# A selective-scan and attention kernel: ScalarE scales the turned dt*u out of PSUM from an earlier unit on, and the fold of Wq and Wk moves to the second image

## The chip, the core and the metric

The kernel runs on one core of a Trainium2 chip. The metric is the device time of one launch in microseconds (us); lower is better. The engines are named as the profile names them: PE is TensorE (matmuls, and PEld its weight loads), DVE is VectorE, ACT is ScalarE, POOL is GpSimd, and SP is the engine whose queue issues the DMAs.

## The reference

Four images of 384 channels and 32x32 positions pass through a state-space layer (four directions k, 16 states per channel) and then through attention and a mixture of four experts. What matters here is the scan and the attention scores:

```python
def step(h, inp):
    dtt, ut, bt, ct = inp
    dA = jnp.exp(dtt[..., None] * A)
    h = h * dA + (dtt * ut)[..., None] * bt[:, :, None, :]
    y = jnp.einsum('bkdn,bkn->bkd', h, ct)
    return (h, y)
...
q = jnp.einsum('btc,ch->bth', x, Wq)
k = jnp.einsum('btc,ch->bth', x, Wk)
wei = jnp.einsum('bth,bsh->bts', q, k) * scale
```

Since q times k transposed is x (Wq Wk^T) x^T, the kernel computes the product of the two weights once. That is the fold.

## The kernel before

**Units and ticks.** The scan is cut into 768 units, 192 for each image (`IMAGE`). A unit is 32 channels times 4 states on the 128 partitions, and 1024 positions along the free dimension. The units of an image run over the channel block m (3), the direction k (4, in two pairs), the group of four states q (4), and the 32-channel block j (4). So 16 units in a row (`EACH`) share one pair (k, m), and four in a row (`NJ`) share one q.

The main loop counts ticks. In tick t it writes out, in this order: `decay(t + 2)` (ACT, L550, the exponential da of the unit after the next), deferred work, `front(t)` (DVE, L557, v = du * B into PSUM), `turned(t + 1)` (PE, L815), `back(t - 1)` (POOL, L570, h * C), `middle(t)` (DVE, L563, the scan), on every fourth tick `row(t - 2)` (PE, L595, the sum over states into y, 16 matmuls), `fetch(t)` (the DMAs of later units), one step of the preparation of an image, and then `go_on`, which steps the generators in the list `side` and the one in `waiting` (attention and experts of the image before). A generator that yields `"wait", n` is not stepped again for n ticks. The order is written out by hand (`manual_schedule`), so each engine executes its instructions in the order in which these ticks issue them, and a tick is a place in that order, not a time. The buffers of da are three, so the da issued in tick t is written only when the scan of unit t - 1 is done. The buffers of v are two.

**Two ways to v.** In the first image, half of the groups of four units (q = 1 and q = 3) can get v in a way that spares DVE. The generator `feed` (L748) loads du of a (k, m) from memory, turns it on PE in 128x128 blocks (L780), copies it from PSUM into the tile dut (ACT, L782), and then lets ACT scale dut by B, 32 instructions of 128x128 for a group of four units (L798), eight of them in a tick, into a tile st. `turned` (L815) then transposes st back on PE, eight transposes a unit, straight into v. `feed` starts a group n0 (its first unit) only if the clock has not passed n0 - 5 (`AHEAD`), and at most two st tiles are alive, so that a group is started from tick n0 - 12 on. A unit that has no st when `turned` is called gets its v from DVE as usual. In the kernel before, the first group so treated is that of unit 36.

**The fold.** `fold` (L706) loads Wq and Wk, turns them (PE L720, ACT L724, six times), multiplies them (PE L730, ACT L735, three times) and stores the result to `g_d` (L738). It is in `side` from tick 0, and its last line appends `feed`. So `feed` begins when the fold has ended. Its tiles come from the pool of st.

**Preparation.** `preparation(b)` normalises image b, projects it (`project_x`, L382), and computes dt and du for each of six (m, pair) in `project_dt` (L407): twice two matmuls into two PSUM banks that must be free in the same tick, a Softplus on ACT for each (with a table load there and one back for Exp), two products on DVE, and four stores. In the first image's ticks there are two such banks (`FIRST_BANKS`) for preparation, fold and `feed` together; the bank's `give` makes it free in the same tick. From tick 192 on there are four, and pools for the attention's tiles (`a0`, `ht`) take the place of that of st.

**What follows an image.** When the last `row` of an image is out, `evict` starts `finish` (layer norm, Gelu, residual), and `behind` waits for it and runs `attention` (L843), which first loads `g_d`, and `experts`.

The call that decides the order of fold and feed is

```python
side.append(later())
side.append(fold())
decay(0)
decay(1)
```

Of the kernel before, what the change touches and what calls it, by code (L numbers as in the profile page):

```python
# [8 lines left out]
F32 = mybir.dt.float32  # L9
AF = mybir.ActivationFunctionType  # L10
# [5 lines left out]
P = 128  # L16
B = 4
C = 384
M = C // P
HW = 32  # L20
L = HW * HW
NH = L // 512
K = 4
N = 16
# [8 lines left out]
NI = P // DJ  # L33
# [16 lines left out]
def hybrid_kernel(  # L50
# [22 lines left out]
    nc = tc.nc  # L73
# [16 lines left out]
    first = ExitStack()  # L90
    pools = {
        "st": first.enter_context(tc.tile_pool(name="stp", bufs=2)),
        "dut": first.enter_context(tc.tile_pool(name="dutp", bufs=1)),
        "v": first.enter_context(tc.tile_pool(name="ps_v", bufs=2, space=PSUM)),
        "pm": ps_m,
    }
# [285 lines left out]
    def project_x(b, pair, u, xd):  # L382

        name = f"bc_{b}_{pair}"
        bc = yield from slots.take(name, P, L)
        mine = slice(64 * pair, 64 * pair + 64)
        other = slice(64 - 64 * pair, 128 - 64 * pair)
        for h in range(NH):
            s = bass.ts(h, 512)
            ps = yield from banks.take(f"pxd_{b}_{pair}_{h}")  # L390
            for c in range(M):
                nc.tensor.matmul(
                    ps, wx[:, c, pair, :], u[c][:, s], start=(c == 0), stop=(c == M - 1)
                )
            yield "wait", 1
            nc.scalar.copy(half(xd[mine, :], h, pair), ps[mine, :].rearrange("p (h w) -> p h w", w=HW))
            rows = half(bc[other, :], h, pair), ps[other, :].rearrange("p (h w) -> p h w", w=HW)
            if b == 0 and pair == 0:
                nc.vector.tensor_copy(*rows)
            else:  # L400
                nc.scalar.copy(*rows)
            banks.give(f"pxd_{b}_{pair}_{h}")
        yield "wait", 1
        nc.sync.dma_start(rows_d[b, pair].rearrange("k j n l -> (k j n) l"), bc[other, :])
        slots.give(name)

    def project_dt(b, pair, m, u, xd):  # L407
# [217 lines left out]
    def layernorm(dst, src, name, lag, b=0, into=None):  # L625
# [77 lines left out]
            banks.give(f"rb_{name}_{h}")  # L703
        return dst

    def fold():  # L706

        raw = pools["st"].tile([P, 2, M, C], F32, tag="st", name="w_raw")
        for j, w in enumerate((wq, wk)):
            nc.sync.dma_start(raw[:, j], w.rearrange("(c p) d -> p c d", p=P))
        wt = pools["st"].tile([P, 2, M, C], F32, tag="st", name="w_t")
        yield "wait", 3
        for j in range(2):
            for d in range(M):
                ps = yield from banks.take(f"pwt_{j}_{d}")
                for c in range(M):
                    nc.tensor.transpose(  # L720
                        ps[:, c * P : (c + 1) * P], raw[:, j, c, d * P : (d + 1) * P], ident
                    )
                yield "wait", 1
                nc.scalar.copy(wt[:, j, d, :], ps[:, :C])  # L724
                banks.give(f"pwt_{j}_{d}")
        g = pools["st"].tile([P, M, C], F32, tag="st", name="g_s")
# [12 lines left out]
        side.append(feed())  # L739

    stored_du = set()
    scaled = {}
    NT = L // P

    def feed():  # L748
        bt = one.tile([P, 2, NT, 4 * N], F32, tag="fx0", name="bt")
        for pair in range(2):  # L750
# [12 lines left out]
            slots.give(f"bt_{pair}")  # L763
        begun = []
        for n in range(0, IMAGE, EACH):
            u = units[n]
            if clock[0] > n + EACH - NJ - AHEAD:
                continue
            while (u["k"], u["m"]) not in stored_du:
                yield "wait", 1  # L770
            name = f"turn_{u['name']}"
            du = yield from slots.take(name, P, L)
            nc.sync.dma_start(du, dts_d[0, u["k"]][1, u["m"] * P : (u["m"] + 1) * P, :])
            yield "wait", 2
            dut = pools["dut"].tile([P, NT, P], F32, tag="dut", name=f"dut_{n}")
            for h in range(2):
                ps = yield from banks.take(f"{name}_{h}")
                for t in range(4):
                    o = (4 * h + t) * P
                    nc.tensor.transpose(ps[:, t * P : (t + 1) * P], du[:, o : o + P], ident)  # L780
                yield "wait", 1
                nc.scalar.copy(dut[:, 4 * h : 4 * h + 4, :], ps.rearrange("p (t d) -> p t d", t=4))  # L782
                banks.give(f"{name}_{h}")
            slots.give(name)
            for q in range(1, NQ, 2):
                n0 = n + q * NJ
                if clock[0] > n0 - AHEAD:
                    continue
                while len(begun) >= 2 and clock[0] < begun[-2] + NJ:

                    yield "wait", 1
                if clock[0] > n0 - AHEAD:
                    continue
                begun.append(n0)
                st = pools["st"].tile([P, NT, NJ * P], F32, tag="st", name=f"st_{n0}")
                for t in range(NT):
                    for i in range(NI):
                        nc.scalar.activation(  # L798
                            st[:, t, :].rearrange("p (d i) -> p i d", i=NI)[:, i, :], dut[:, t, :],
                            AF.Copy,  # L800
                            scale=bt[:, u["pair"], t, u["i"] * 2 * N + q * NI + i :][:, :1],
                        )
                    if t % 2:
                        yield "wait", 1
                scaled[n0] = st

    def turned(n):

# [32 lines left out]
            defer(1 + m // 2, add)  # L841

    def attention(b, yb, fx0):  # L843
        gw_ = []
        for name, w in ((f"wg_{b}", g_d), (f"wv_{b}", wv.rearrange("(c p) d -> p c d", p=P))):
            ta = yield from slots.take(f"{name}a", P, 2, C)
# [433 lines left out]
    assert clock[0] < -2  # L1280
    clock[0] = -2
    side.append(later())
    side.append(fold())
    decay(0)
    decay(1)
    t = 0
    while t < NU + 4 or waiting or side or due or inner or parked:
        clock[0] = t
        if t + 2 < NU:
            decay(t + 2)  # L1290
        for f in due.pop(t, []):
# [78 lines left out]
```

## Time and profile before

The median of three runs is 3821.93 us (3818.68 to 3824.02). The profiled execution took 3819.22 us, with a span of 3817.4 us.

| stretch of the span | what runs | us | DVE busy | ACT busy | PE busy | granted PE clock |
|---|---|---|---|---|---|---|
| 49.37 to 171.99 | units 0 to 31 | 122.62 | 116.02 | 70.64 | 69.73 | 0.64 |
| 171.99 to 715.92 | units 32 to 191 | 543.93 | 493.31 | 462.10 | 344.07 | 0.69 |
| 715.92 to 781.50 | first units of the second image | 65.58 | 63.88 | 37.94 | 41.56 | 0.68 |

The stretches begin and end at the start of a scan (L563). Each engine's share says how much of a stretch it had an instruction in work; it says nothing of whether another engine waited for it. Over the whole span, 768 scans took 1751.6 us of DVE, 688 products v another 854.3 us, and 640 scaling instructions (L798) were put down with 498 ns each in the median. In 80 units, then, v was made by way of st.

An entry such as "DVE h L563 <- PE v L815: 20.2, 16, 3.7" in a view of waits means that the scan stood idle for 20.2 us in total, 16 times, 3.7 us at the longest, until the transposes of line 815 released it.

### The profile page before, as it was taken

The numbers are of one execution on the slowest core, as the hardware profiler recorded it, in microseconds if no ns is written. First come the engines' busy times: TensorE is split into PE (matmuls) and PEld (weight loads), VectorE is DVE, ScalarE is ACT, GpSimd is POOL, SyncE is SP. The second block draws the span as 40 slices with busy tenths as digits, with TensorE's granted clock in tenths as the row PEclk, the third lists the DMA queues.
The fourth block names the chain that finished last, engine by engine and source line by source line (L and its number), as shares of the span: only waits on it lengthen the run. The fifth ranks groups of instructions, "written<-read, shape, count | busy, mean of one in ns | idle before, by whom it ended". The sixth has DMA issues, their size and how long they took to land.

```text
span 3817.4 us, 33900 instructions
## 1 busy us (share of the span) xinstructions
PE 3373.4 (88%) x11367; PEld 1498.2 (39%) x11367; DVE 2993.1 (78%) x2094; ACT 2104.3 (55%) x2695; POOL 1816.5 (48%) x776
## 2 busy tenths in 40 slices
PE   4665666679999999799999999789999999999999
PEld 1123322235334334345333343354343434644444
DVE  6999899999899999989988999999999992210000
ACT  4688888555666656556565555455555552422121
POOL 2677677645555555545555565455666560000000
PEclk7677766689999999899999999899999999999999
DMA  6565556445576666536756656346566551222321
GB/s 205 204 224 177 213 203 219 171 167 186 179 247 227 222 238 226 178 120 209 239 195 224 214 194 208 136 151 208 200 205 235 188 181 38 90 73 84 94 84 52
DMA packets 407838, 678.26 MB, mean 178 GB/s; under 512 B 33472, under 2 KB 280560, under 8 KB 407664
## 3 DMA queue, kind: packets, MB, share of 16 engines
q1 hardware_dynamic: 401456, 675.70, 51.9%
q8 instruction: 90, 1.47, 0.2%
q10 hardware_dynamic: 6208, 0.39, 0.1%
q14 instruction: 84, 0.69, 0.1%
HBM read 604.04 MB, written 71.96 MB: 177 GB/s over the span
## 4 chain that ended last, share of the span: by engine, by line
PE 42%; DVE 34%; ACT 6%; issue 5%; DMA 1%; POOL 1%; DVEq 0%; SPq 0%; POOLq 0%; ACTq 0%
DVE h L563 21%; PE ph L1154 15%; PE fy L1179 15%; DVE v L557 10%; PE y L595 4%; ACT da L550 2%; PE pq L868 2%; PE pv L879 2%; PE ss L897 1%; ACT st L798 1%; PE po L963 1%; DVE fy L1188 1%; POOL h L570 1%; PE v L815 1%; DMA du<-dts 1%
## 5 line engine op out<-in xcount | busy, mean ns | idle before, releaser
L570 POOL TENSOR_TENSOR h<-h,bc 128x1024 f32<-128x1024 f32 x768 | 1815.5, 2367 | 1330.7 <-DVE v L557 1099.3
L563 DVE TENSOR_TENSOR_SCAN h<-da,v 128x1024 f32<-128x1024 f32 x768 | 1751.6, 2284 | 106.4 <-PE v L815 20.2
L550 ACT ACTIVATE da<-dt,a 128x1024 f32<-128x1024 f32 x768 | 876.1, 1146 | 940.9 <-DVE h L563 892.0
L1154 PE MATMUL ph<-fx,w 128*128 128x512 f32 x2304 | 1020.7, 599 | 7.3 <-DMA w<-in_w 3.2
L1179 PE MATMUL fy<-ht,w 128*128 128x512 f32 x2304 | 1023.2, 601 | 0.9 <-ACT dt L429 0.9
L557 DVE TENSOR_TENSOR v<-du,bc 128x1024 f32<-128x1024 f32 x688 | 854.3, 1242 | 35.8 <-DMA du<-dts 16.3
L1179 PEld LDWEIGHTS fy<-ht,w 128*128 128x128 f32 x2304 | 437.4, 192 | 577.0 <-issue 550.0
L1154 PEld LDWEIGHTS ph<-fx,w 128*128 128x128 f32 x2304 | 433.5, 191 | 581.6 <-issue 533.5
L595 PE MATMUL y<-h,sel 128*32 128x512 f32 x3072 | 536.7, 675 | 140.5 <-POOL h L570 140.5
L1139 ACT ACTIVATE ht<-ph,b1s 128x512 f32<-128x512 f32 x384 | 257.6, 678 | 456.7 <-PE ph L1154 455.9
L1188 DVE SCALAR_TENSOR_TENSOR fy<-fy,b2s,tw 128x512 f32<-128x512 f32 x96 | 72.2, 752 | 426.1 <-PE fy L1179 426.1
L595 PEld LDWEIGHTS y<-h,sel 128*32 128x32 f32 x3072 | 102.0, 117 | 481.3 <-POOL h L570 252.2
L815 PE MATMUL v<-ident,st 128*128 128x128 f32 x640 | 134.3, 381 | 97.9 <-DVE h L563 96.3
L798 ACT ACTIVATE st<-dut,bt 128x128 f32<-128x128 f32 x640 | 205.1, 501 | 0.1
L1143 ACT ACTIVATE ht<-ht 128x3072 f32<-128x3072 f32 x64 | 176.8, 2763 | 0.8
L815 PEld LDWEIGHTS v<-ident,st 128*128 128x128 f32 x640 | 109.2, 199 | 161.2 <-issue 86.2
L550 ACT ACT_TABLE_LOAD x110 | 141.1, 1283 | 14.5 <-DMA dt<-dts 11.5
L423 PE MATMUL pdt<-xd,wdt 12*128 12x512 f32 x184 | 84.2, 819 | 66.4 <-ACT dt L429 34.9
L963 PE MATMUL po<-pt,vt 128*128 128x256 f32 x480 | 106.1, 370 | 7.8 <-ACT pt L859 7.8
L897 PE MATMUL ss<-axn,qt 128*128 128x512 f32 (+3 forms) x288 | 100.5, 493 | 3.1 <-ACT pr L915 2.7
L963 PEld LDWEIGHTS po<-pt,vt 128*128 128x128 f32 x480 | 93.8, 196 | 23.4 <-ACT pt L859 10.0
L911 DVE TENSOR_REDUCE nb<-ss 128x1 f32<-128x512 f32 (+3 forms) x48 | 25.9, 552 | 75.3 <-PE ss L902 61.0
(201 smaller groups left out, 1642.6 us busy)
## 6 DMA issues: line engine op xcount, KB each, us to landing
bc<-rows SPq DMA_DIRECT2D x384, 512.0 KB, 4.7
w<-in_w SPq DMA_DIRECT2D x384, 384.0 KB, 6.0
dt<-dts SPq DMA_DIRECT2D x192, 512.0 KB, 4.0
du<-dts SPq DMA_DIRECT2D x192, 512.0 KB, 6.6
dts<-dt SPq DMA_DIRECT2D x48, 512.0 KB, 3.5
dts<-du SPq DMA_DIRECT2D x48, 512.0 KB, 3.7
fx<-t2d SPq DMA_DIRECT2D x12, 768.0 KB, 6.4
tw<-mkd SPq DMA_DIRECT2D x32, 256.0 KB, 6.5
```

The costliest lines, as they stand in the source:

```text
L550: nc.scalar.activation(u["da"], spread["dt4", n], AF.Exp, scale=a4[:, g, u["q"] : u["q"] + 1])
L557: return nc.vector.tensor_tensor(u["v"], spread["du4", n], spread["bc", n][:, 0, :], ALU.mult)
L563: nc.vector.tensor_tensor_scan(u["h"][:, ::step], u["da"][:, ::step], u["v"][:, ::step], 0.0, op0=ALU.mult, op1=ALU.add,)
L570: product = nc.gpsimd.tensor_tensor(h, h, spread["bc", n][:, 1, :], ALU.mult)
L595: nc.tensor.matmul(y, sel, h, start=first, stop=last, tile_position=(0, jj * DJ))
L798: nc.scalar.activation(st[:, t, :].rearrange("p (d i) -> p i d", i=NI)[:, i, :], dut[:, t, :], AF.Copy, scale=bt[:, u["pair"], t, u["i"] * ...
L815: nc.tensor.transpose(u["v"][:, t * P : (t + 1) * P], st[:, t, u["j"] * P : (u["j"] + 1) * P], ident)
L963: nc.tensor.matmul(pv[:, o:], vt[:, j, m * P : (m + 1) * P], pts[step][j // 4][:, j % 4, o:], start=False, stop=(j == nj - 1),)
L1139: nc.scalar.activation(ht[:, f, :], ps, AF.Identity, bias=bias)
L1143: nc.scalar.activation(ht, ht, AF.Gelu)
L1154: nc.tensor.matmul(ps, tiles[n][:, c, (f % 2) * P : (f % 2 + 1) * P], xns[h][:, c, :], start=(c == 0), stop=(c == M - 1),)
L1179: nc.tensor.matmul(pss[m], tiles[n][:, f, :], hts[fh][:, f, :], start=(fh == 0 and f == 0), stop=(fh == 1 and f == FH - 1),)
```

## The change

Four edits, made together:

1. `feed` is put into `side` at the start in place of `fold`. It waits for its own inputs instead: `stored_rows` says that the projected rows of a pair are stored, and each pair's rows are turned when they are first needed (`turn_rows`).
2. The tile dut and its copy are gone. For each group q, du is turned again on PE into a bank, four blocks at a time, and ACT scales the blocks out of that bank. The first bank is held over one tick of waiting and two of scaling, the second is taken in the middle of the first one's scaling if it is free. The slot with du is held until both groups of a (k, m) are done.
3. `fold` is put into `side` at tick 192. Its tiles come from the pool `ht`, it waits two ticks for its loads in place of three, and it ends by noting itself in `folded`.
4. `attention` waits until `folded` is set.

```diff
+        if b == 0:
+            stored_rows.add(pair)
...
-        raw = pools["st"].tile([P, 2, M, C], F32, tag="st", name="w_raw")
+        def square(name):
+            t = pools["ht"].tile([P, M, L], F32, tag="ht", name=name)
+            t = t.rearrange("p m l -> p (m l)")[:, : 2 * M * C]
+            return t.rearrange("p (j c d) -> p j c d", j=2, c=M)
+
+        raw = square("w_raw")
...
-        yield "wait", 3
+        wt = square("w_t")
+        yield "wait", 2
...
-        side.append(feed())
+        folded.append(1)
...
-            dut = pools["dut"].tile([P, NT, P], F32, tag="dut", name=f"dut_{n}")
-            for h in range(2):
-                ps = yield from banks.take(f"{name}_{h}")
+
+            def dut(q, h, du=du, name=name):
+                ps = banks.now(f"{name}_{q}_{h}")
                 for t in range(4):
                     o = (4 * h + t) * P
                     nc.tensor.transpose(ps[:, t * P : (t + 1) * P], du[:, o : o + P], ident)
-                yield "wait", 1
-                nc.scalar.copy(dut[:, 4 * h : 4 * h + 4, :], ps.rearrange("p (t d) -> p t d", t=4))
-                banks.give(f"{name}_{h}")
-            slots.give(name)
+                return ps
...
-                for t in range(NT):
-                    for i in range(NI):
-                        nc.scalar.activation(
-                            st[:, t, :].rearrange("p (d i) -> p i d", i=NI)[:, i, :], dut[:, t, :],
-                            AF.Copy,
-                            scale=bt[:, u["pair"], t, u["i"] * 2 * N + q * NI + i :][:, :1],
-                        )
-                    if t % 2:
+                ps = [None, None]
+                for h in range(2):
+                    if ps[h] is None:
+                        while not banks.ready():
+                            yield "wait", 1
+                        ps[h] = dut(q, h)
                         yield "wait", 1
+                    for t in range(4):
+                        for i in range(NI):
+                            nc.scalar.activation(
+                                st[:, 4 * h + t, :].rearrange("p (d i) -> p i d", i=NI)[:, i, :],
+                                ps[h][:, t * P : (t + 1) * P], AF.Copy,
+                                scale=bt[:, u["pair"], 4 * h + t, u["i"] * 2 * N + q * NI + i :][:, :1],
+                            )
+                        if t == 1:
+                            if h == 0 and banks.ready():
+                                ps[1] = dut(q, 1)
+                            yield "wait", 1
+                    banks.give(f"{name}_{q}_{h}")
+                    yield "wait", 1
                 scaled[n0] = st
+            slots.give(name)
...
     def attention(b, yb, fx0):
+        while not folded:
+            yield "wait", 1
...
-    side.append(fold())
+    side.append(feed())
...
             second()
+            side.append(fold())
```

More of the change, by code (lines that the diff above doesn't have):

```diff
@@ L92, in hybrid_kernel @@
         "st": first.enter_context(tc.tile_pool(name="stp", bufs=2)),
-        "dut": first.enter_context(tc.tile_pool(name="dutp", bufs=1)),
         "v": first.enter_context(tc.tile_pool(name="ps_v", bufs=2, space=PSUM)),
@@ L704, in layernorm @@
         return dst
+    folded = []
     def fold():
-        raw = pools["st"].tile([P, 2, M, C], F32, tag="st", name="w_raw")
+        def square(name):
[3 more added lines that the diff above has]
+        raw = square("w_raw")
         for j, w in enumerate((wq, wk)):
             nc.sync.dma_start(raw[:, j], w.rearrange("(c p) d -> p c d", p=P))
-        wt = pools["st"].tile([P, 2, M, C], F32, tag="st", name="w_t")
-        yield "wait", 3
+        wt = square("w_t")
+        yield "wait", 2
         for j in range(2):
@@ L725, in fold @@
                 banks.give(f"pwt_{j}_{d}")
-        g = pools["st"].tile([P, M, C], F32, tag="st", name="g_s")
+        g = square("g_s")[:, 0]
         for m in range(M):
@@ L738, in fold @@
         nc.sync.dma_start(g_d, g)
-        side.append(feed())
+        folded.append(1)
+    stored_rows = set()
     stored_du = set()
@@ L749, in feed, with turn_rows @@
         bt = one.tile([P, 2, NT, 4 * N], F32, tag="fx0", name="bt")
-        for pair in range(2):
+        def turn_rows(pair):
+            while pair not in stored_rows:
+                yield "wait", 1
             rows = yield from slots.take(f"bt_{pair}", 4 * N, L)
@@ L764, in feed @@
         begun = []
+        yield from turn_rows(0)
         for n in range(0, IMAGE, EACH):
@@ L768, in feed @@
                 continue
+            if u["pair"] == 1 and u["m"] == 0 and u["i"] == 0:
+                yield from turn_rows(1)
             while (u["k"], u["m"]) not in stored_du:
@@ L843, in attention @@
     def attention(b, yb, fx0):
+        while not folded:
+            yield "wait", 1
         gw_ = []
```

## The prediction

> **What bounds the kernel now.** I first read the busy shares on the page, then the groups of instructions of the two stretches in which the change acts, the waits of DVE and ACT there, the chain of waits, and last the timeline of one turned group.
>
> Groups of instructions on DVE, for units 0 to 31 (first two lines) and 32 to 191 (last two): count, busy us, mean ns, idle before them.
>
> ```profile
> L563 DVE TENSOR_TENSOR_SCAN h<-da,v 128x1024 f32<-128x1024 f32 x33 | 75.5, 2287 | 4.6 <-DVE v L557 0.5
> L557 DVE TENSOR_TENSOR v<-du,bc 128x1024 f32<-128x1024 f32 x32 | 40.5, 1267 | 1.7 <-DMA du<-dts 1.7
> ...
> L563 DVE TENSOR_TENSOR_SCAN h<-da,v 128x1024 f32<-128x1024 f32 x161 | 364.6, 2281 | 41.6 <-PE v L815 20.2 <-ACT da L550 6.9 <-POOL h L570 3.0
> L557 DVE TENSOR_TENSOR v<-du,bc 128x1024 f32<-128x1024 f32 x80 | 103.1, 1288 | 3.3 <-DMA bc<-rows 2.6 <-DMA du<-dts 0.5
> ```
>
> DVE sets the pace in both. In the first stretch it is busy 116.0 of 122.6 us and each unit costs it a scan and a product: where nothing else runs, scans start 3.6 us apart. In the second, half of the units have no product, and DVE stands idle some 50 of 543.9 us, mostly for the transposes of line 815 and for ACT's da.
>
> ACT in the first stretch, and then its scaling, copying and turning rows in the second:
>
> ```profile
> L550 ACT ACTIVATE da<-dt,a 128x1024 f32<-128x1024 f32 x34 | 38.9, 1147 | 53.3 <-DVE h L563 44.8 <-DMA dt<-dts 8.3
> ...
> L798 ACT ACTIVATE st<-dut,bt 128x128 f32<-128x128 f32 x624 | 199.9, 501 | 0.1
> ...
> L782 ACT COPY dut<-turn 128x512 f32<-128x512 f32 x18 | 10.2, 566 | 0.2 <-PE turn L780 0.2
> ...
> L780 PE MATMUL turn<-ident,turn 128*128 128x128 f32 x72 | 10.7, 295 | 3.7 <-DMA turn<-dts 3.7
> ```
>
> ACT idles 53 of 122.6 us in the first stretch, nearly always until a scan frees a da buffer: that is room. The 501 ns is a latency. The timeline of one turned group shows the pace:
>
> ```profile
> 479.53 2.56 ACT L798 ACTIVATE st<-dut,bt 128x128 f32<-128x128 f32 x8
> 482.12 1.15 ACT L550 ACTIVATE da<-dt,a 128x1024 f32<-128x1024 f32 x1
> 483.17 2.56 ACT L798 ACTIVATE st<-dut,bt 128x128 f32<-128x128 f32 x8
> 483.42 8.91 DVE L563 TENSOR_TENSOR_SCAN h<-da,v 128x1024 f32<-128x1024 f32 x4
> 487.94 1.97 PE L815 MATMUL v<-ident,st 128*128 128x128 f32 x8 [0.21 <-DVE h L563]
> 489.84 2.46 PE L595 MATMUL y<-h,sel 128*32 128x512 f32 x16
> 492.24 1.09 PE L815 MATMUL v<-ident,st 128*128 128x128 f32 x8
> 493.47 2.29 DVE L563 TENSOR_TENSOR_SCAN h<-da,v 128x1024 f32<-128x1024 f32 x1 [1.13 <-PE v L815]
> ```
>
> Eight scalings take 2.56 us, 0.32 each, so they overlap; a group of four units costs ACT 4 x 2.5 = 10 us. Turned units can follow each other at the scan's own 2.2 us, until PE's row of y (2.46 us) comes between two units' transposes and DVE waits 1.13 us. So a spared product (1.32 us with its gap, 3.6 - 2.28) is not earned in full.
>
> The chain that ended last, cut to units 32 to 191 (it reaches back to about 382 us):
>
> ```profile
> by line: DVE h L563 16.4%; ACT st L798 7.7%; issue 6.1%; ACT da L550 6.1%; DVE v L557 5.7%; PE v L815 4.6%; PE y L595 3.5%; DMA du<-dts 3.1%; ACT L429 1.7%; ACT dt L429 1.5%; ACT L550 1.4%; DVE du L437 1.1%; PE pdt L423 0.5%; ACT ut L415 0.
> ```
>
> ACT's scaling holds 7.7% of 543.9, 42 us: there ACT has the last word for part of the time.
>
> **What the Trainium skill says.** Perfetto Trace Analysis, section "Optimizing Scalar/DVE Operations", puts ScalarE's access overhead at about 93 ns on SBUF and 51 ns on PSUM, profiled latency being about twice that. The trace fits in part: the PSUM copy of 512 (566 ns) has 566 - 427 = 139 ns beyond its elements, at the 0.833 ns an element of ScalarE: Activation LUTs, section "What ACT_TABLE_LOAD costs"; that section gives 186 ns plus elements for an instruction with immediates and about 93 ns per pointer operand, and da (1024, one pointer, SBUF) shows 1142 - 853 = 289. PSUM — Partial Sum Buffer, section "Engine vs sequencer instructions", says that ScalarE's and VectorE's queues are strictly first in, first out and that matmuls start and complete in program order; nothing in the trace speaks against it, and the 1.13 us above is such a case.
>
> **Part 1: feed starts at tick 0.** I followed ticks by hand. Rows and du are turned by tick 5; the preparation holds both banks in ticks 4 and 5, so the group of unit 12 gets its bank at tick 6, is scaled in ticks 7 to 10 and noted in tick 11, just after `turned(12)` was called. So unit 12 may still go to DVE, and 13 to 15 are turned. Groups 20 and 28 start at ticks 13 and 18 and are in time. Group 36 now meets the preparation of the second pair of rows (ticks 28 to 30) and may lose its first unit. Gain: 10 units net (12 at most). What is one worth? Unturned, units 32 to 191 would need 160 x (3.62 + 0.23) = 616 us, where 3.62 is the quiet spacing and 0.23 the rest of DVE's work (about 36.6 us / 160); they took 543.9 with 80 turned, so each turned unit earned 0.90 us. 10 x 0.90 = 9.0 us. ACT must carry 12 chunks more among units 5 to 31: 12 x 2.5 = 30 us, less 4.2 us of fold (6 x 0.460 + 3 x 0.470), in 53 us of idleness. It fits, but not in ticks 4 to 8, where Softplus, its table loads and the ut copy leave ACT no gap; the delay there is the reason why I don't take the full 1.32.
>
> **Part 2: scaling out of PSUM.** Gone are 22 dut copies, 22 x 0.566 = 12.5 us of ACT. Added are turns: 23 groups x 8 = 184 against 88. Four take 0.63 us, so about 15 us more of PE. The trace has no strided small read of PSUM. By the page's 42 ns a chunk of eight could be 0.34 us cheaper; if the write with its 16-byte stride limits the pace, nothing. A price above today's I exclude on the read side, as PSUM reads in the trace are not slower than SBUF reads of their size. I take 0.15 us: 6% of the chain's 42 us is 2.5, and since the chain covers only 334 of 543.9 us, 4 us in all. The copies lie on no listed piece of the chain: nothing. New is that ACT's chunk waits for PE in the same group: behind ACT's instruction stand the da of the next ticks and the preparation's Softplus, for which DVE's scans and du products wait. When a group starts at tick n0 - 12, its turns fall in ticks 0 and 1 of eight, the transposes to v in ticks 3 to 6, so PE has time. Only when the preparation holds the banks do the turns slip into the transposes. PE's lines hold some 8.6% of 543.9 against the chain's 61%, 14%; 14% of 15 us is 2 us lost. Bounds for all of part 2: -10 to +12 us (half a microsecond a group). I take -2.
>
> **Part 3: the fold goes.** At the start its two loads (576 KB each, issued at 50.6 and 52.1) share the DMA engines with du of unit 2, for which DVE idles 1.3 us; rows of 256 KB and, five ticks in, du take their place. Gain 1.0 us. In the second image's ticks 192 to 204 it adds 4.2 us to ACT, 18 turns and 27 matmuls (3.5 + 8.1 us) to PE, two loads and a store to SP's queue. DVE is busy 63.9 of 65.6 us there and ACT waits for it, so this is beside other work; with the cover gone it would be 4.2 us. PE may stand some 2 us for Wq (10.5 us to landing against two ticks), with nothing on DVE waiting for it. I take +1.0.
>
> **Part 4: attention's wait.** `fold` ends near tick 204, about 765 us by the present clock; attention loads `g_d` at 778.27 us today. No wait: 0. If banks delayed the fold by four ticks, it would cost a tick, 4 us.
>
> Sum: -9.0 - 2.0 - 1.0 + 1.0 = -11.0 us. Later images run the same program, so the gain lasts to the end. From 3819.22 that is 3808.2; the median of the runs shown lies 2.7 us above the profiled one, which gives 3811.
>
> **Rivals.** *ACT full early.* Between units 5 and 31 ACT gets no idle time any more, and da arrives late for what DVE saves. For it: no gap on ACT from 58 to 80 us. Against it: 53 us idle after all. The new groups earn nothing: -2, about 3820; the same time results if feed misses its ticks and turns no more units. *ACT was the bound.* The 12.5 us of copies and the full 0.34 us for each of 92 chunks count, half of these 44 us ends on the path: -22 with the 12 units, 3798. *PE and the two banks.* This is the slower one: feed holds a bank nearly all the time, so turns and the preparation's matmuls wait for each other's banks on ACT, and PE, in order, brings v late. Its place is each of the 23 groups, its price the turns of one group, 2 x 0.63 = 1.3 us, 29 us in all; against 11 us gained, 3840. It decides from 0.5 us a group on. For it: 20.2 us of DVE's idleness already is PE's v. Against it: PE is idle a third of the stretch.
>
> **Chances.** Forecast 0.52, ACT full early 0.24, ACT the bound 0.10, PE and banks 0.14. A measurement of this kernel tells about 0.2% (7.6 us) from no change. The forecast falls short of that in few cases (0.02), the first rival nearly always. Faster 0.60, within 0.26, slower 0.14. The range runs from the second rival (3796) to just past the first (3825); the forecast's own is 3803 to 3818.
>
> **What would show it.** Right: about 678 products on L557 (676 if unit 12 is in time), 736 scalings with chunks of 2.3 to 2.5 us, units 0 to 31 in about 113 us, units 32 to 191 in about 542, no wait of attention. Wrong: DVE waiting for PE's v or ACT's da well over 27 us in the first image, or chunks longer than 2.56 us.

## The result, and the profile after

The changed kernel takes 3795.53 us in the median of four runs (3792.43 to 3799.20), and the kernel before, beside it on the same chip, 3822.56. The ratio is 0.993, with a 95% interval of 0.9918 to 0.9942: faster, by 27 us where 11 were forecast, and half a microsecond below the lower end of the range that the prediction gave. The profiled executions stand 24.2 us apart (spans of 3817.4 and 3793.2 us).

From the page of the kernel after, the groups that count products and scalings (count, busy us, mean ns of one, idle before them):

```profile
L558 DVE TENSOR_TENSOR v<-du,bc 128x1024 f32<-128x1024 f32 x678 | 841.7, 1241 | 38.8 <-DMA du<-dts 21.7
...
L819 ACT ACTIVATE st<-turn,bt 128x128 f32<-128x128 f32 x736 | 213.6, 532 | 0.1
```

688 products have become 678, and 640 scalings 736: the change does what was followed by hand. The next two lines are the stretches of the kernel after that answer to the table of before, cut at the same scans; the columns are length, busy time of PE, weight loads, DVE, ACT and POOL, granted PE clock, DMA share and GB/s:

```profile
49.03:165.55 116.52, 67.76 (x278) 28.68 (x278) 103.65 (x60) 94.79 (x170) 73.66 (x31) 0.70 0.67 238
165.55:680.71 515.16, 325.02 (x1528) 163.83 (x1528) 479.63 (x268) 422.61 (x879) 381.04 (x160) 0.74 0.58 212
```

| units | before, us | after, us | difference | forecast |
|---|---|---|---|---|
| 0 to 31 | 122.6 | 116.5 | -6.1 | -10.0 |
| 32 to 191 | 543.9 | 515.2 | **-28.7** | -2.0 |
| 192 to 239 (fold, attention) | 219.2 | 219.8 | +0.6 | +1.0 |
| 240 to 287 | 212.1 | 223.9 | **+11.8** | 0 |
| 288 to 351 | 262.4 | 261.8 | -0.6 | 0 |

From unit 352 on the two executions differ by about 1 us in total. So two things were not foreseen: 27 us more than forecast in units 32 to 191, and 12 us given back in the second image. One execution is not exact to a microsecond: experiments 4 and 8 below leave the first image's instructions as they are here, and in their profiles units 32 to 191 took 517.3 and 516.8 us.

Where did the 28.7 us come from? DVE's groups in units 32 to 191, first after, then the two groups of du of the kernel before:

```profile
L564 DVE TENSOR_TENSOR_SCAN h<-da,v 128x1024 f32<-128x1024 f32 x160 | 361.6, 2280 | 34.3 <-PE v L841 22.0 <-POOL h L571 1.1 <-ACT da L551 0.6
L558 DVE TENSOR_TENSOR v<-du,bc 128x1024 f32<-128x1024 f32 x81 | 103.8, 1281 | 1.0 <-DMA du<-dts 0.6 <-DVE h L564 0.3
L438 DVE TENSOR_TENSOR du<-dt,x 128x1024 f32<-128x1024 f32 x8 | 10.3, 1288 | 0.0
L438 DVE TENSOR_TENSOR du<-dt,ut 128x1024 f32<-128x1024 f32 x7 | 8.8, 1256 | 0.0
```

```profile
L437 DVE TENSOR_TENSOR du<-dt,ut 128x1024 f32<-128x1024 f32 x8 | 16.0, 1996 | 3.0 <-ACT dt L429 3.0
L437 DVE TENSOR_TENSOR du<-dt,x 128x1024 f32<-128x1024 f32 x8 | 13.4, 1675 | 1.0 <-ACT dt L429 1.0
```

Scans and products v are nearly as before. But the products du of the preparation, which no line of the change touches, fell from means of 1.7 and 2.0 us to under 1.3, and their idle time to nothing. DVE is busy 13.7 us less (493.3 to 479.6), of which these two groups make 10.3 (29.4 to 19.1, with one product fewer in the stretch), and idle 15 us less. What DVE waited for there, before:

```profile
DVE h L563 <- PE v L815: 20.2, 16, 3.7
DVE h L563 <- ACT da L550: 6.9, 7, 1.7
DVE du L437 <- ACT dt L429: 4.0, 6, 1.4
```

and after:

```profile
DVE h L564 <- PE v L841: 22.0, 17, 3.8
DVE h L564 <- POOL h L571: 1.1, 2, 0.6
DVE h L564 <- ACT da L551: 0.6, 1, 0.6
DVE v L558 <- DMA du<-dts: 0.6, 2, 0.3
```

The wait for PE stays, those for ACT are gone (in the profile of experiment 4, with the same instructions here, 2.9 us for da and 2.0 for st are back). On ACT, the copies (18 in the stretch, 10.2 us) are gone, and the scalings in units 32 to 191 take 183.7 us where they took 199.9. A run of eight took 2.24 to 2.49 us, 2.28 in the median of 92, where it was 2.56 before. From the start of one scaling to the start of the next there were 250 ns in place of 293. Two such runs in the timeline:

```profile
80.08 2.28 ACT L819 ACTIVATE st<-turn,bt 128x128 f32<-128x128 f32 x8
86.15 2.40 ACT L819 ACTIVATE st<-turn,bt 128x128 f32<-128x128 f32 x8
```

One of the long products du of the kernel before, in its timeline, lines of other engines left out:

```profile
510.99 1.26 ACT L429 ACTIVATE dt<-pdt,dtb 128x512 f32<-128x512 f32 x2
...
511.32 2.36 POOL L570 TENSOR_TENSOR h<-h,bc 128x1024 f32<-128x1024 f32 x1 [1.00 <-DVE h L563]
...
511.71 3.06 DVE L437 TENSOR_TENSOR du<-dt,ut 128x1024 f32<-128x1024 f32 x1 [0.53 <-ACT dt L429]
512.14 2.56 ACT L798 ACTIVATE st<-dut,bt 128x128 f32<-128x128 f32 x8
514.69 2.27 DVE L563 TENSOR_TENSOR_SCAN h<-da,v 128x1024 f32<-128x1024 f32 x1
```

DVE waits 0.53 us for Softplus. In that time POOL begins its product h * C, at 511.32. The product du then starts on paper at 511.71, but ends at 514.77, when POOL has been done since 513.68: 3.06 us for work that takes 1.2. That it ends about 1.1 us after POOL's end is what the Trainium skill, SBUF — State Buffer, section "Who interferes with whom", describes: a DVE instruction with two inputs in SBUF and a GpSimd instruction that reads SBUF contend for a shared read interface, which is locked, and the order of issue decides which of the two blocks. The trace agrees: the six products du of this stretch that took over 2 us (five of 3.0 to 3.1, one of 2.1) all began after POOL's product, behind an idle gap of 0.5 to 1.4 us in which POOL had begun; the ten without a gap took 1.2 to 1.3 us. In this kernel it happens where v comes from ACT and PE. Where DVE makes v, the code lets POOL's product wait for it (`order` in `back`); without a product v, POOL's product starts as soon as the scan is done.

That gave two theories, neither of them shown by the two profiles alone. **Relief:** ACT has less to do (copies gone, scalings cheaper), so dt, da and st come sooner. **Place:** `feed` now holds the two banks at other ticks, and so the steps of `project_dt`, which must find both banks free in one tick, fall elsewhere in the period of eight ticks, where they disturb DVE less.

### The profile page after: what moved, and what is told of

Read it like the earlier page. It is cut to its first block, busy times and chain, and to the rows that moved or that the text cites. A ratio compares the mean times of both kernels' runs of the same rounds, so it can differ in the third digit from the quotient of the medians.

```text
span 3793.2 us, 34275 instructions
## 1 busy us (share of the span) xinstructions
PE 3366.5 (89%) x11543; PEld 1518.3 (40%) x11543; DVE 2964.4 (78%) x2084; ACT 2089.9 (55%) x2767; POOL 1815.1 (48%) x776
## 4 chain that ended last, share of the span: by engine, by line
DVE 42%; PE 40%; ACT 7%; issue 6%; DMA 3%; POOL 1%; DVEq 0%; SPq 0%; POOLq 0%; ACTq 0%
DVE h L564 25%; PE ph L1182 13%; PE fy L1207 13%; DVE v L558 12%; PE y L596 4%; ACT da L551 2%; PE ss L925 2%; PE pq L896 2%; PE pv L907 2%; PE v L841 1%; PE pxd L391 1%; ACT st L819 1%; DVE du L438 1%; DMA du<-dts 1%; PE po L991 1%
## 5 line engine op out<-in xcount | busy, mean ns | idle before, releaser
L558 DVE TENSOR_TENSOR v<-du,bc 128x1024 f32<-128x1024 f32 x678 | 841.7, 1241 | 38.8 <-DMA du<-dts 21.7
L596 PE MATMUL y<-h,sel 128*32 128x512 f32 x3072 | 493.8, 661 | 101.4 <-POOL h L571 101.3
L596 PEld LDWEIGHTS y<-h,sel 128*32 128x32 f32 x3072 | 97.4, 116 | 412.2 <-issue 219.8
L841 PE MATMUL v<-ident,st 128*128 128x128 f32 x720 | 143.1, 364 | 110.6 <-DVE h L564 110.6
L819 ACT ACTIVATE st<-turn,bt 128x128 f32<-128x128 f32 x736 | 213.6, 532 | 0.1
```

Of the source, the lines that this page charges most:

```text
L558: return nc.vector.tensor_tensor(u["v"], spread["du4", n], spread["bc", n][:, 0, :], ALU.mult)
L596: nc.tensor.matmul(y, sel, h, start=first, stop=last, tile_position=(0, jj * DJ))
L819: nc.scalar.activation(st[:, 4 * h + t, :].rearrange("p (d i) -> p i d", i=NI)[:, i, :], ps[h][:, t * P : (t + 1) * P], AF.Copy, scale=bt[ ...
L841: nc.tensor.transpose(u["v"][:, t * P : (t + 1) * P], st[:, t, u["j"] * P : (u["j"] + 1) * P], ident)
```

## The experiments

In all of them "place" is the tick, modulo 8, in which the first product du of a step of `project_dt` stands, read off the order of instructions. Units whose v comes from ACT have their scans in ticks 4 to 7 of eight. The steps from unit 48 to 191 stand in places 4, 5, 2, 3, 4, 5, 6 before and in places 2, 3, 1, 2, 3, 0, 1 after. One more, at tick 35 before, stands at the start of the stretch; after, it is at tick 31, just ahead of the stretch. Places given below are those from unit 48 on, too, where nothing else is said.

**1. The work of ACT put back, the ticks kept.** In the kernel after, each bank is copied to SBUF and scaled from there: 46 copies over the image, and no cheaper scaling.

```diff
+                    held_ = pools["dut"].tile([P, 4, P], F32, tag="dut", name=f"dut_{n0}_{h}")
+                    nc.scalar.copy(held_, ps[h].rearrange("p (t d) -> p t d", t=4))
...
-                                ps[h][:, t * P : (t + 1) * P], AF.Copy,
+                                held_[:, t, :], AF.Copy,
```

> The kernel after, with one copy put back: each bank of turned du is first copied to SBUF by ACT (46 copies of 128x512) and scaled from there; every tick of the program stays where it is, banks held as long. Theory A (ACT relieved): units 32 to 191 go from 515 back to 532 us or more, and DVE waits for ACT's da and dt again (10 us and more). Theory B (the held banks move the preparation's du products to ticks where DVE is not locked out): 522 us or less, du products stay at 1.2 to 1.4 us each.

Measured: 3808.91 us (ratio 0.9958, 0.9941 to 0.9974). Units 32 to 191 took 526.8 us, between what the two theories expected. Its ACT groups and its stretch:

```profile
L822 ACT ACTIVATE st<-dut,bt 128x128 f32<-128x128 f32 x638 | 204.9, 501 | 1.3
...
L819 ACT COPY dut<-turn 128x512 f32<-128x512 f32 x39 | 22.0, 565 | 0.1
```

```profile
166.06:692.90 526.84, 330.01 (x1528) 165.05 (x1528) 479.72 (x268) 461.03 (x923) 381.17 (x160) 0.72 0.57 208
```

ACT is as busy as before the change (461.0 against 462.1 us), and yet 17 of the 28.7 us remain, DVE's busy time (479.7) with them. What the copies and the slower scaling cost here is 11.7 us against the kernel after, and 9.6 to 10.1 against experiments 4 and 8. So relief is worth some 10 to 12 us, of which 7.5 lie in ticks 88 to 111, where ACT also normalises the second image (79.4 us after, 86.9 here).

**2. The steps moved in the kernel before.** The pause between the steps is cut from 12 ticks to 11.

```diff
-                yield "wait", 0 if b == 0 and m == 0 else 12
+                yield "wait", 0 if b == 0 and m == 0 else 11 if b < 2 else 12
```

> The kernel before, with the preparation's pause of 12 ticks made 11 for the first two images, so that its du products fall in ticks 2 and 6 of eight in place of 2 to 6, drifting. Theory A: units 32 to 191 stay at 538 to 546 us (543.9 before). Theory B: 520 to 530 us, no du product over 2 us.

Measured: 3832.42 us (1.0022, 1.0015 to 1.0028), units 32 to 191 in 548.7, slower than either theory expected. The steps now stand in place 2 twice and then in place 6 six times; the last of them is one more than the stretch held before. The products du are cheap here (1.2 us), so the exclusion of DVE and POOL is not what makes place 6 bad. The timeline of one step in place 6 shows the other half:

```profile
594.58 0.79 ACT L798 ACTIVATE st<-dut,bt 128x128 f32<-128x128 f32 x2
...
595.16 1.12 ACT L550 ACTIVATE da<-dt,a 128x1024 f32<-128x1024 f32 x1
...
596.30 1.28 ACT L429 ACT_TABLE_LOAD   x1
...
597.59 1.26 ACT L429 ACTIVATE dt<-pdt,dtb 128x512 f32<-128x512 f32 x2
...
598.33 2.65 PE L423 MATMUL pdt<-xd,wdt 12*128 12x512 f32 x4 [2.50 <-ACT dt L429]
...
600.91 1.97 PE L815 MATMUL v<-ident,st 128*128 128x128 f32 x8
...
603.02 2.29 DVE L563 TENSOR_TENSOR_SCAN h<-da,v 128x1024 f32<-128x1024 f32 x1 [4.77 <-PE v L815]
```

Read from the bottom: DVE idles 4.77 us before the scan, until v is there. PE transposes v only from 600.91, since the second half of the step's matmuls stands ahead of it in its queue. These waited 2.50 us for a bank that Softplus empties, and Softplus stood on ACT behind scaling, da and a table load. Where v comes from DVE, no scan waits for PE's transposes, so such a delay should cost DVE less; the table below bears that out.

**3. Scaling out of PSUM alone.** The kernel before with the second edit only; `fold` is still first, and `feed` late. The pauses for the second image are 10 instead of 12.

```diff
-            dut = pools["dut"].tile([P, NT, P], F32, tag="dut", name=f"dut_{n}")
...
+                        ps[h] = dut(q, h)
...
-                yield "wait", 0 if b == 0 and m == 0 else 12
+                yield "wait", 0 if b == 0 and m == 0 else 10 if b == 1 else 12
```

> The kernel before with the scaling out of PSUM alone (feed still after the fold, fold at the start; the preparation's pause is 10 ticks for the second image, since its slots run out otherwise). If the gain among units 32 to 191 belongs to this edit, they take 512 to 522 us here too; if it comes from the earlier start of feed or the fold's move, 535 us or more. Units 0 to 31 as before, 122 us.

Measured: 3813.05 us (0.997, 0.996 to 0.998), units 0 to 31 in 123.0 and units 32 to 191 in 529.2. The early start isn't there, and 14.7 us of the 28.7 are: less than expected if this edit made the whole gain, more than expected if it made none. DVE waits 8.6 us for DMA here (0.6 after, 3.1 before), which is part of what is missing. The steps stand in places 0, 1, 1, 0, 0, 0, 0, behind a first one at tick 39, in place 7.

**4. The last preparation step three ticks earlier.** This is about the 12 us given back: in the kernel after, the second image's last pause is cut.

```diff
-                yield "wait", 0 if b == 0 and m == 0 else 12
+                yield "wait", 0 if b == 0 and m == 0 else 9 if b == 1 and m == M - 1 and pair == 1 else 12
```

> The kernel after, with the last pause of the second image's preparation 9 ticks in place of 12, so that the third image's preparation begins in the tick it had before. If the 12 us given back among units 240 to 351 come from its later projection, they return: about 3784 us. If they come from the fold or from the granted clock, the time stays at 3795 within 3 us.

Measured: 3788.54 us (0.9905, 0.9889 to 0.9921). Units 240 to 351 take 478.2 us: 485.7 after, 474.5 before. Some 7.5 of 11.1 us are back.

**5. Exclusion in the kernel before.** `feed`'s scaling of a group and the Softplus ticks of a step take turns.

```diff
+        while busy:
+            yield "wait", 1
+        busy.append(m)
         for h in range(NH):
...
+        busy.clear()
         yield "wait", 1
...
+                while busy:
+                    yield "wait", 1
+                busy.append(n0)
                 st = pools["st"].tile([P, NT, NJ * P], F32, tag="st", name=f"st_{n0}")
...
+                    if t == NT - 1:
+                        busy.clear()
```

> The kernel before, with nothing but a lock in the order of the program: the preparation's Softplus ticks and feed's four scaling ticks exclude each other, as the held banks make them do in the kernel after. ACT's work is that of before, all of it. If the exclusion carries the gain among units 32 to 191, they take 522 to 532 us in place of 543.9; if ACT's relief carries it, 538 us or more.

Measured: 3829.12 us (1.002, 1.0013 to 1.0027). Units 32 to 191 take 533.3 us, 10.6 less than before, with the old scaling and all the copies, and just short of what was expected of exclusion; but units 192 to 383 take 832.9 against 818.8, and that eats it.

**6. The change without scaling out of PSUM.** Start of `feed`, move of `fold` and attention's wait as in the kernel after; dut and its copy as before.

```diff
+            dut = pools["dut"].tile([P, NT, P], F32, tag="dut", name=f"dut_{n}")
...
-                                ps[h][:, t * P : (t + 1) * P], AF.Copy,
+                            st[:, t, :].rearrange("p (d i) -> p i d", i=NI)[:, i, :], dut[:, t, :],
```

> The kernel after without the scaling out of PSUM: feed starts at once and the fold is in the second image, but du is turned and copied once for 16 units and scaled from SBUF, with the banks free again at once. If that edit made the gain, units 32 to 191 take 536 to 548 us; if the earlier start or the fold's move did, 522 or less. Units 0 to 31 (one turned group less than after): 115 to 120 us.

Measured: 3827.31 us (1.0016, 1.0008 to 1.0025). Units 0 to 31 take 116.1 us, so the early start is earned there, but units 32 to 191 take 549.5 (with 704 scalings over the image, one group fewer than after) and units 192 to 239 take 230.2 (219.2 before). What DVE waits for in units 32 to 191:

```profile
DVE h L565 <- PE v L833: 40.3, 22, 6.9
DVE v L559 <- DMA bc<-rows: 4.6, 2, 4.3
```

Steps stand in places 6 (at tick 46), 7, 4, 5, 6, 7, 0.

**7. The same with the exclusion of experiment 5.**

> e6 with the lock of e5. Exclusion carries the gain: units 32 to 191 in 518 to 530 us, at least 10 below e6. Relief carries it: within 4 us of e6.

Measured: 3807.26 us (0.996, 0.9945 to 0.9976), units 32 to 191 in 521.3, as expected of exclusion:

```profile
165.66:686.95 521.29, 316.98 (x1456) 156.57 (x1456) 482.50 (x266) 451.60 (x895) 379.66 (x160) 0.70 0.58 212
```

That is 28 us below experiment 6, with the same scalings (202.1 us of ACT) and the same 18 copies. The wait for PE's v is 19.0 us. Steps stand in places 1, 2, 7, 0, 1, 2, 3. A rule about ticks alone thus makes 28 of the 34 us that lie between experiment 6 and the kernel after.

**8. The last pause gone altogether** (kernel after, 0 in place of the 9 of experiment 4).

> The kernel after, with no pause at all at the end of the second image's preparation, so that the third image is projected some ten ticks earlier, beside the attention and ahead of the experts' matmuls. If what was given back is projection work pushed into the stretch where PE is the bound, units 240 to 351 take 478 us or less (485.7 after, 478.1 with a pause of 9) and the total 3786 us or less. If only the exact tick mattered, 485 us and 3795.

Measured: 3789.31 us (0.9912, 0.9897 to 0.9926), 3 us more than expected. Units 240 to 351 take 472.9 us, as expected, but units 192 to 239 now 222.7 in place of 219.8. Units 240 to 287, first before, then after, then this one:

```profile
935.14:1147.25 212.11, 203.03 (x661) 83.56 (x660) 193.53 (x150) 132.82 (x134) 113.22 (x48) 0.98 0.64 216
```

```profile
900.47:1124.36 223.89, 212.83 (x677) 88.04 (x677) 193.86 (x151) 135.07 (x138) 113.12 (x48) 0.96 0.60 204
```

```profile
905.41:1114.36 208.95, 199.17 (x630) 81.75 (x629) 191.25 (x148) 117.99 (x121) 113.25 (x48) 0.96 0.64 219
```

PE is busy 203 of 212 us before: here PE, with the experts' matmuls, is the bound. The groups of PE in this stretch hold 12 matmuls of the third image's projection before and 24 after:

```profile
L392 PE MATMUL pxd<-x,wx 128*128 128x512 f32 x12 | 5.6, 599 | 0.0
...
L391 PE MATMUL pxd<-x,wx 128*128 128x512 f32 x24 | 12.8, 678 | 0.0
```

In this experiment there is none, as all 24 stand before unit 240, beside DVE-bound work. The granted clock is 0.96 here as in the kernel after, so it is not what was lost.

**9. Exclusion, and the pauses cut to 10, in the kernel before.** To tell exclusion from place.

```diff
-                yield "wait", 0 if b == 0 and m == 0 else 12
+                yield "wait", 0 if b == 0 and m == 0 else 10 if b < 2 else 12
```

> The kernel before with the lock of e5 and the preparation's pause at 10 ticks for the first two images. From group 92 on feed scales in the very ticks of the kernel before, and ACT has all the work it had; only the preparation's Softplus now falls in ticks 5 and 6 of eight and its du products in 7 and 0, outside of the scaling and of the turned units. If the collision of the two was what units 32 to 191 paid for, they take 516 to 526 us (543.9 before, 533.3 in e5), although nine preparations in place of eight and a half fall among them, and the total is 3795 to 3806 us. If ACT's load counts most, 536 us or more.

Measured: 3821.94 us (1.0005, 0.9996 to 1.0014), units 32 to 191 in 539.6: the expectation failed. Scaling and Softplus don't meet, the products du take 1.24 us, and the steps still cost much. They stand in places 4, 3, 7, 7, 7, 7, 7, 6; that is one step more than before the change. DVE waits:

```profile
DVE h L568 <- PE v L825: 29.5, 19, 3.1
DVE h L568 <- ACT dt L433: 5.9, 3, 2.6
```

So the theory had to be mended: it isn't that scaling and Softplus meet, but where the step as a whole stands against the ticks in which v comes from PE.

**10. PE's row of y a tick later.** On top of experiment 8, to move the y matmuls out from between two units' transposes.

```diff
-        for half in range(NH):
-            for jj in range(NJ):
+        for jj in range(NJ):
+            for half in range(NH):
...
-        if t >= 2 and t - 2 < NU and (t - 2) % NJ == NJ - 1:
-            row(t - 2)
+        late = 3 if t < IMAGE and t % EACH % (2 * NJ) in (5, 6) else 2
+        if t >= late and t - late < NU and (t - late) % NJ == NJ - 1:
+            row(t - late)
```

> e8 with the row of y that falls among four turned units issued one tick later, behind the last unit's transposes, and its matmuls ordered so that the oldest h is read first. If that row is what keeps PE's v late once the collisions are gone (DVE's 24 us in e8), units 32 to 191 fall from 516.8 to 500 to 510 us and the total to 3775 to 3783. If the h buffer that the row then holds becomes the new wait, 515 us or more.

Measured: 3813.93 us (0.9983, 0.9976 to 0.999), units 32 to 191 in 527.9: the hope failed, and what was expected of the h buffers came. Units 0 to 31 are slower as well (122.4 us, 115.8 in experiment 8).

```profile
DVE h L564 <- PE y L596: 32.3, 20, 2.9
DVE h L564 <- PE v L841: 5.6, 2, 2.9
```

The wait for v falls from 24.1 us in experiment 8 to 5.6, and a new one takes its place: the scan now waits for the row to free one of the seven tiles h. An eighth tile was not tried.

**11. Place alone, in the kernel before.** Exclusion as in experiment 5, pauses of 10, and a step may begin only in ticks that bring its first product du to place 1.

```diff
-        while busy:
+        while busy or 24 < clock[0] < IMAGE and clock[0] % 8 != 6:
             yield "wait", 1
```

> The kernel before, all its ACT work and its SBUF scaling kept, with the order of the preparation alone changed: from tick 25 on a dt step starts only in tick 6 of eight and not beside a scaling, so that its first du product comes in tick 1 of eight. By the sixteen-tick stretches of the runs so far, a dt step costs DVE 4 to 7 us when its first du product comes in ticks 4 to 7 of eight and 2 to 4 us in ticks 0 to 3, whichever memory ACT scales from. If that place is the cause, units 32 to 191 take 516 to 526 us and the total is 3795 to 3806. If ACT's relief is needed, 534 or more.

Measured: 3804.30 us (0.9953, 0.9938 to 0.9968), units 32 to 191 in 522.7, both as expected. Its stretch, its scans and its ACT work:

```profile
171.06:693.79 522.73, 323.39 (x1442) 154.74 (x1442) 486.10 (x272) 462.20 (x911) 375.70 (x160) 0.69 0.58 210
```

```profile
L568 DVE TENSOR_TENSOR_SCAN h<-da,v 128x1024 f32<-128x1024 f32 x161 | 364.1, 2281 | 31.1 <-PE v L825 14.5 <-ACT da L555 3.7 <-ACT st L806 1.4
```

ACT is as busy as before the change, to 0.1 us, `fold` is first, `feed` late, and no scaling comes out of PSUM. Still 21.2 of the 28.7 us are there. Experiment 9 is the same kernel without the rule on places: the rule alone takes 539.6 to 522.7 us (one step of the preparation, at tick 190, has left the stretch with it). The granted clock is 0.69, as before the change, where the kernel after had 0.74, so these 21 us do not come from the clock either.

**12. The same rule in the kernel after**, with pauses of 10 and none at the end.

```diff
+        while b < 2 and 24 < clock[0] < IMAGE and clock[0] % 8 != 6:
+            yield "wait", 1
```

> The kernel after with the same rule (a dt step starts in tick 6 of eight) and without the last pause of e8. Place of the dt steps as the cause: some 1 us gained for each of seven steps against e8, units 32 to 191 in 505 to 513 us, total 3778 to 3786. If the held banks had already put the steps as well as can be: 515 to 518 us, 3786 to 3792.

Measured: 3788.67 us (0.9912, 0.9895 to 0.9928), units 0 to 31 in 111.8 and units 32 to 191 in 519.9. It is no faster than experiments 4 and 8, the second of its two expectations: the held banks already keep the steps out of the bad places (from unit 48 on, all 14 steps of the kernel after and of experiment 3 stand in places 0 to 3), and one more step stands in the stretch (it left units 0 to 31, which got 4.7 us shorter). The three kernels at 3788.5 to 3789.3 us are faster than the kernel before and, by some 6 us, than the changed one (ratios 0.9905 to 0.9912 against 0.993; the intervals overlap a little).

**What a step costs DVE, by its place.** I took the scan-to-scan gaps in the nine ticks around the first product du (four on either side), less the median gap of undisturbed ticks of the same place in all runs. Left out are steps that meet the second image's normalisation (ticks 88 to 111), those ahead of tick 48, where `feed` makes its first groups, and experiment 10.

| place | scaling from SBUF, us | scaling from PSUM, us |
|---|---|---|
| 0 | 2.8 to 4.1 | 3.0 to 4.2 |
| 1 | 1.9 to 3.2 | 1.9 to 3.0 |
| 2 | 3.6 to 4.6 | 2.9 to 4.7 |
| 3 | 1.8 to 5.7 | 1.7 to 2.9 |
| 4 | 2.4 to 7.5 | none |
| 5 | 7.4 to 7.6 | none |
| 6 | 5.9 to 7.7 | none |
| 7 | 5.5 to 7.1 | none |

Where both columns have entries, the row counts more than the column. Place is not all: place 4 goes from 2.4 to 7.5, and the steps left out at ticks 34 and 35 cost 6 to 7 us in places 2 and 3.

A sum that needs no median says the same. The first column is what units 48 to 87 and 112 to 191 took, that is the stretch without its start and without the normalisation; the others are the start and the normalisation.

| kernel | 48 to 87 and 112 to 191, us | 32 to 47, us | 88 to 111, us |
|---|---|---|---|
| before | 405.2 | 55.2 | 83.6 |
| after | 385.1 | 50.7 | 79.4 |
| experiment 1 (ACT's work put back) | 387.3 | 52.6 | 86.9 |
| experiment 6 (no PSUM) | 400.3 | 55.7 | 93.4 |
| experiment 7 (no PSUM, exclusion) | 385.7 | 48.2 | 87.4 |
| experiment 9 (before, exclusion) | 400.5 | 55.1 | 84.1 |
| experiment 11 (before, place) | 385.1 | 55.0 | 82.5 |

So 20.1 of the 28.7 us lie in the first column, and order alone brings all of them: experiment 11 has the same 385.1 us with ACT's work of before. Another 4.5 us lie in the start, which the step of tick 35 has left for tick 31 (52.3 and 52.7 us in experiments 8 and 4, so it is nearer 3), and 4.2 in ticks 88 to 111. There ACT's relief counts: its work put back costs 7.5 us in these ticks, and 2.2 in the first column. How order and relief share the 4.2 us was not separated. The two overlap: 21.2 us for order in experiment 11 and 11.7 for relief in experiment 1 make more than 28.7.

## Why the prediction was wrong in size, point by point

**Counts and ticks: right.** Unit 12 and one unit of group 36 were missed, and 678 products and 736 scalings came as worked out. A run of eight came out cheaper than taken: 2.28 us in the median, where 2.41 follow from 2.56 less 0.15. The 43 ns from start to start are all of the 42 ns that the prediction gave as the bound and of which it counted less than half.

**Part 1, -9.0 and -1.0 for the start: -6.1 measured.** The ten products are earned on DVE (116.0 to 103.65 us busy). Idle time grew by 6.3 us, though: 7.7 us are now spent waiting for PE's v, 5.2 of them at the scans of units 30 and 31. With the preparation's second pair at ticks 28 to 30 I saw only what it does to `feed` (one unit lost), not that a step of the preparation, at tick 35 before, has its first product du at tick 31 now, inside this stretch, in place 7. In experiment 12, where it comes at tick 36, the stretch takes 111.8 us, 10.8 less than before. The 1.0 us for the start was not there: the wait of unit 2 for du went from 1.3 to 1.8 us.

**Part 2, -2.0 for units 32 to 191: -28.7 measured; this is the step that failed.** The prediction took the two banks for something that only delays `feed` ("Only when the preparation holds the banks do the turns slip into the transposes"), charged 2 us for the turns on PE, and in the slower rival 29 us. What the longer hold does to the place of the preparation's steps has no term in the sum: it stood at nothing, without a reason. `feed` holds the banks longer and in other ticks, and the preparation's steps wait until both are free. That moved the steps out of most of the ticks in which v comes from PE, and it is worth some 20 us. Experiments 7 and 11 show it with no scaling out of PSUM; experiment 6 shows that without it the early start earns nothing over the first image (665.6 us, 666.6 before). Nothing in the change aims at good places, so this part of the gain is luck, and the forecast had the sign right for another reason.

The 4 us taken for relief on ACT were small as well: experiment 1 makes relief some 10 to 12 us. In time it came nearest to the rival "ACT was the bound" (3798), but not in cause: 17 of 28.7 us stay with ACT as full as ever. That rival's own sum doesn't lead to 3798 either: half of 44 us taken from 3822 gives 3800, and about 3790 with the turned units.

The profile of before had the sign of it: products du of 1.7 and 2.0 us where products v of the same size took 1.29. I counted them as "the rest of DVE's work" and asked for no reason.

**Part 3, +1.0: +0.6 measured**, which is within what two executions differ by. The fold lies beside DVE's work as expected. **Part 4, 0: 0.** The fold stores `g_d` at 732.9 us, and attention loads it at 743.1.

**"Later images run the same program, so the gain lasts to the end": wrong by 11.8 us.** The steps that wait for banks end the second image's preparation three ticks later (its last step stands at tick 202, 199 before), so the third image's projection comes some three to five ticks later too, and half of it more falls into units 240 to 287, where PE is the bound. Experiments 4 and 8 return 7.5 and 12.8 us of units 240 to 351 by ending the preparation sooner, which shows the cause; experiment 8 pays 2.9 us of it in units 192 to 239. Why experiment 4, with the projection in the ticks of before, keeps 3.6 us was not followed.

## What to carry to other kernels

A bank, slot or tile that two generators share is also a clock: whoever holds it longer decides when the other's work is written out, so for every edit that changes how long it is held, follow the other one's ticks too, past the end of the stage. Ask of a group that is slower than its twin of the same shape (here du at 2.0 us and v at 1.3) where in the order it stands before it is booked as fixed work. And to tell whether a gain comes from less work or from another order, put the work back while the order stays (experiment 1), and change the order while the work stays (experiment 11).

## What the runs showed of the hardware that wasn't expected

- A 128x1024 product of two SBUF inputs on DVE took 3.06 us instead of 1.2 when POOL's product (2.36 us) had begun 0.39 us sooner; five such products (3.0 to 3.1 us) and one of 2.1 us stood in units 32 to 191 of the kernel before, and none in the kernel after. The other way round, POOL's product took 3.2 to 3.3 us where DVE's had begun 0.15 us sooner.
- Eight scalings of 128x128 blocks, written with a stride of 16 bytes, took ACT 2.28 us out of PSUM against 2.56 out of SBUF, and 250 ns against 293 from start to start, though the recorded mean of one rose (501 to 528 ns): latency and pace moved in opposite directions.
- Eight PE transposes for which the profile names no wait of their own began 5.1 us after the work of PE before them had ended: matmuls ahead of them in PE's queue waited 2.50 us for a bank and then took 2.65 (experiment 2), and DVE stood idle 4.77 us. It is the case that the prediction cited of the Trainium skill, PSUM — Partial Sum Buffer, section "Engine vs sequencer instructions": matmuls start and complete in program order.
